# One-hots four groups ahead, transposes two groups ahead, the dense stage in pieces of six products: a graph kernel on one core

## The chip, the cores and the metric

The kernel runs on one core of one Trainium2 chip. The metric is device time in microseconds (us), the median of several timed runs, without the profiler. A profile is one further execution with the hardware profiler recording; its time is given apart wherever it is used.

## The reference

A graph of 6250 nodes (rows of 256 float32 values) and 100,000 edges, each with a source, a destination and one of 8 types. The edges come sorted by destination, and destinations are 6250 u² for uniform u, so low node numbers have many more edges than high ones. Three relational graph layers, then a layer norm, an attention stage and another layer norm:

```python
for l in range(3):
    xr = jnp.einsum('nd,rde->rne', x, W_rel[l])          # 8 matrices of 256x256
    msg = xr[edge_type, src]                             # 100000 x 256
    agg = jax.ops.segment_sum(msg, dst, num_segments=6250)
    x = relu(agg + x @ W_root[l] + bias[l])
x = layernorm(x_in + x)
# attention: for the first 6250 edges, softmax over 4 heads of leaky_relu(alpha_l + alpha_r),
# times the transformed row of the edge's destination, summed over heads, copied to all heads
x = layernorm(x + attention(x))
```

The sum over a node's edges and the product with W_rel can be swapped: first add up, for every destination and type, the source rows, then multiply each of the 8 sums by its matrix. The kernel does that.

## The kernel before, in words

**Tables.** At the start `tables()` turns the edge lists into tables in SBUF: `idx` (the source of each edge), `key` (the column of an edge's type and destination within its tile's window) and `pos` (where a tile's window lies). The edges make 782 tiles of 128. Four consecutive tiles are a *group* (`GT = 4`); a layer has 197 groups, and one step of its loop, `i`, handles one.

**What a step does with a group.** GpSimd fetches the source rows of each tile by an indirect DMA of 128 rows of 1 KB (`gather`, L425), four of them per group, into one of 8 message buffers (`mp`, `bufs=8`). VectorE compares an iota with the keys and so makes the *one-hot* matrices of the group's four tiles in one operation (`onehot`, L409), each 128 edges by 8 types x W destinations; W falls from 26 to 6 along the edge list, since low nodes have more edges per node. TensorE multiplies message by one-hot (`windows`, L442): per tile two products, one for each half of the 256 features, which add up the rows of all edges with the same destination and type in a PSUM bank (`ps_w`, five banks). VectorE adds each tile's result into the ring `S[f]` at a run-time offset (`add`, L454). An fp32 matmul appears in the trace as two records, so a group of four tiles makes 16 window records.

**Two rings.** The edge tiles are split into two halves. `S[0]`, for the upper half of the edges, holds the sums of 4 node tiles of 128 nodes; `S[1]`, for the lower half, holds 3. A group of the upper half touches ring 0, one of the lower half ring 1. `pl.order()` interleaves the two, from the end of each half backwards. Which one-hots are wide differs: in the profile's shapes, a window of a tile has 208 to 144 columns in the one half and 144 to 48 in the other. One node tile is shared between both halves: its part from the lower half is kept aside (`hold`).

**The dense stage.** When the last group that can reach a node tile has been added (`ready`), the tile's row block `xin` has been fetched (`load_rows`), is transposed on TensorE (`turn`, L477) and copied to SBUF by ScalarE as `xT` (L479). In the next step, right behind the next windows, `dense` does 18 products with 256 columns: 2 with W_root (L504) and 16 with W_rel (L507), all into the one PSUM bank `pd`; they are 36 records. One step later `finish` adds the bias (L519), applies relu (L522) and stores the rows in DRAM, where the next layer's gathers read them, and ScalarE clears the tile's place in the ring (`clear`, L514). At most one node tile is handled by `dense` in a step. There are 49 node tiles, so 147 dense tiles in the three layers.

**Order.** The three layers run under a manual schedule: each engine carries out its instructions in the order in which the program emits them, and waits where an operand isn't ready. In the loop's order a step emits: row loads, gathers, position loads on VectorE, the one-hot of the *next* group, `finish` of the tile done in the step before, this group's windows, the dense stage of a tile, this group's adds, and the turn of a tile that has just become ready:

```python
    for i in range(NG + 5):
        ...
        nxt = onehot(i + 1) if i + 1 < NG else None
        ...
            wins = windows(i, msg, oh)
        for f, j, xT in turned[:1]:
            fin.append((f, j, dense(f, j, xT)))
        turned = turned[1:]
        if i < NG:
            add(i, wins, vals)
```

The list `done[f]` names the node tiles whose dense stage has been emitted. An add to a ring declares that it has no conflict with their dense reads if its window lies in other node tiles of the ring; the offset is known only at run time, so an add without that declaration is ordered behind every earlier read of the ring, and a later read behind it.

After the three layers comes `attention()`, which the change doesn't touch.

Of the kernel before, what the change touches and what calls it, by code (L numbers as in the profile page):

```python
# [10 lines left out]
F32 = mybir.dt.float32  # L11
# [8 lines left out]
P = 128  # L20
# [2 lines left out]
NS = (4, 3)  # L23
PAD = 32
MARGIN = 800
LEAD = 6
GWIN = 256
GK = 8
# [3 lines left out]
class Plan:  # L32
# [29 lines left out]
    def order(self):  # L62
# [3 lines left out]
        b = [[t for t in k if t < self.TM] for k in g if k[0] < self.TM]  # L66
        n = max(1, len(b) - LEAD)
        seq, k = [], 0
# [7 lines left out]
    def high(self, t):  # L76
        return max(self.N * ((P * (t + 1) + MARGIN) / self.E) ** 2, 127.0)

    def low(self, t):
        return self.N * (max(0.0, P * t - MARGIN) / self.E) ** 2 - 1.0  # L80

# [48 lines left out]
def fast(tc, const, pl, x, xs, src, dst, edge_type, w_rel, w_root, bias, weight,  # L130
         attn_l, attn_r, out, flag):
    nc = tc.nc
    N, D = x.shape
    E = src.shape[0]
    L, R = w_rel.shape[0], w_rel.shape[1]
    H, DH = attn_l.shape
    KC = D // P
    NT, T, CH, WMAX = pl.NT, pl.T, pl.CH, pl.WMAX
    KR = KC * R

    with ExitStack() as top:
        tab = top.enter_context(tc.tile_pool(name="tab", bufs=1))
        ident = tab.tile([P, P], F32, name="ident")
        idx = tab.tile([P, CH * P], I32, name="idx")
        key = tab.tile([P, CH * P], F32, name="key")
        pos = tab.tile([1, CH * P], I32, name="pos")
        iota_p = tab.tile([P, 1], F32, name="iota_p")
        eps = tab.tile([P, 1], F32, name="eps")
        bias_b = tab.tile([P, L, D], F32, name="bias_b")
        w1x = tab.tile([P, KC, D + 2 * H], F32, name="w1x")  # L150
        altab = tab.tile([P, NT, H], F32, name="altab")

        psi = top.enter_context(tc.tile_pool(name="psi", bufs=1, space=PSUM))
        iota = psi.tile([P, R * WMAX], F32, name="iota")

        dram = top.enter_context(tc.tile_pool(name="lanes", bufs=1, space=DRAM))
        lane = dram.tile([NT * P], I32, name="lane")
        with tc.tile_pool(name="ps_p", bufs=2, space=PSUM) as ps_p:
            tables(tc, pl, ps_p, src, dst, edge_type, ident, idx, key, pos, iota, iota_p,
                   lane, flag, R, H)  # L160
        y = dram.tile([NT * P, D], F32, name="y")

        with ExitStack() as s:
            wp = s.enter_context(tc.tile_pool(name="wp", bufs=2))
            sp = s.enter_context(tc.tile_pool(name="sp", bufs=1))
            mp = s.enter_context(tc.tile_pool(name="mp", bufs=8))
            op = s.enter_context(tc.tile_pool(name="op", bufs=3))
            xp = s.enter_context(tc.tile_pool(name="xp", bufs=3))
            ps_w = s.enter_context(tc.tile_pool(name="ps_w", bufs=5, space=PSUM))
            ps_d = s.enter_context(tc.tile_pool(name="ps_d", bufs=1, space=PSUM))  # L170
            ps_t = s.enter_context(tc.tile_pool(name="ps_t", bufs=1, space=PSUM))


            S = [sp.tile([P, KR, n * P + PAD], F32, name=f"S{f}") for f, n in enumerate(NS)]

            hold = {j: sp.tile([P, KR, P], F32, name=f"hold{j}") for j in sorted(pl.shared(pl.TM))}

            nc.vector.memset(eps, EPS)
            for t in S:
                nc.scalar.memzero(t)  # L180
            nc.sync.dma_start(bias_b, bias.rearrange("l d -> (l d)").partition_broadcast(P))
            fold_weights(tc, xp, w1x, weight, attn_l, attn_r)

            def load_w(l):
                wr = wp.tile([P, KC, R, D], F32, name="wr")
                wo = wp.tile([P, KC, D], F32, name="wo")
                for k in range(KC):
                    nc.scalar.dma_start(
                        wr[:, k], w_rel[l, :, k * P:(k + 1) * P, :].rearrange("r p e -> p r e"))
                    nc.scalar.dma_start(wo[:, k], w_root[l, k * P:(k + 1) * P, :])  # L190
                return wr, wo

            groups = pl.order()

            ready = {}
            for i, (f, g) in enumerate(groups):
                for j in pl.reach(g):
                    ready[f, j] = i

            with tc.manual_schedule():  # L200
                nxt = load_w(0)
                for l in range(L):
                    wr, wo = nxt
                    if l + 1 < L:
                        nxt = load_w(l + 1)
                    layer(tc, pl, l, l == L - 1, groups, ready, S, hold, idx, key, pos, iota, ident,
                          wr, wo, bias_b, x, xs, eps, w1x, altab, y,
                          mp, op, xp, ps_w, ps_d, ps_t, H)

        attention(tc, pl, lane, dst, idx, iota_p, ident, eps, w1x, altab, y, out, H)  # L210
# [178 lines left out]
def layer(tc, pl, l, final, groups, ready, S, hold, idx, key, pos, iota, ident, wr, wo, bias_b, x, xs,  # L389
          eps, w1x, altab, y, mp, op, xp, ps_w, ps_d, ps_t, H):  # L390
    nc = tc.nc
    N, D = x.shape
    KC = D // P
    R = wr.shape[2]
    NT = pl.NT
    LAST = N - (NT - 1) * P
    NG = len(groups)
# [4 lines left out]
    def rows(j):  # L402
        return P if j < NT - 1 else LAST

    def onehot(i):
        g = groups[i][1]
        w = R * pl.W[g[0] // P]
        oh = op.tile([P, GT, R * pl.WMAX], F32, name="oh")
        nc.vector.tensor_tensor(  # L409
            oh[:, :len(g), :w], iota[:, :w].unsqueeze(1).to_broadcast([P, len(g), w]),  # L410
            key[:, g[0]:g[-1] + 1].unsqueeze(2).to_broadcast([P, len(g), w]), ALU.is_equal)
        return oh
# [51 lines left out]

    def load_rows(j):
        n = rows(j)
        t = xp.tile([P, D], F32, name="xin")
        if n < P:
            nc.vector.memset(t, 0.0)
        nc.sync.dma_start(t[:n], table[j * P:j * P + n, :])  # L470
        return t

    def turn(t):

        pt = ps_t.tile([P, 4 * P], F32, name="pt")
        for k in range(KC):
            nc.tensor.transpose(pt[:, k * P:(k + 1) * P], t[:, k * P:(k + 1) * P], ident)  # L477
        xT = xp.tile([P, KC, P], F32, name="xT")
        nc.scalar.copy(xT.rearrange("p k n -> p (k n)"), pt[:, :D])  # L479
        return xT  # L480

# [16 lines left out]
        clear(1, j)  # L498

    def dense(f, j, xT):  # L500
        pd = ps_d.tile([P, 512], F32, name="pd")
        s = cols(f, j)
        for k in range(KC):
            nc.tensor.matmul(pd[:, :D], xT[:, k], wo[:, k], start=(k == 0), stop=False)  # L504
        for k in range(KC):
            for r in range(R):
                i = nc.tensor.matmul(pd[:, :D], s[:, k * R + r], wr[:, k, r],  # L507
                                     start=False, stop=(k == KC - 1 and r == R - 1))
                tc.add_to_no_dep_group(f"used{l}_{f}_{j}", i.ins)
        done[f].append(j)  # L510
        return pd

    def clear(f, j):
        i = nc.scalar.memzero(cols(f, j))  # L514
# [38 lines left out]
    last = {}  # L553
# [2 lines left out]
            last[j] = (i, f)  # L556
    fetch = {}
    for j, (i, f) in last.items():
        fetch.setdefault(max(0, i - 3), []).append(j)
    held, turned = {}, []  # L560
    oh = onehot(0)
    fin, log = [], []
    for i in range(NG + 5):
        for j in sorted(fetch.get(i, []), reverse=True):
            held[j] = load_rows(j)
        if i < NG:
            msg = gather(i)
            vals = places(i)
        nxt = onehot(i + 1) if i + 1 < NG else None
        for j, yt in [t for k, t in log if k <= i - 2]:  # L570
            logits(j, yt)
        log = [(k, t) for k, t in log if k > i - 2]
        for f, j, pd in fin:
            yt = finish(j, pd)
            clear(f, j)
            if final:
                log.append((i, (j, yt)))
        fin = []
        if i < NG:
            wins = windows(i, msg, oh)  # L580
        for f, j, xT in turned[:1]:
            fin.append((f, j, dense(f, j, xT)))
        turned = turned[1:]
        if i < NG:
            add(i, wins, vals)
        for f, j in sorted((k for k, r in ready.items() if r == i), key=lambda k: -k[1]):
            fold(f, j)
            if f == 1 and j in late:
                keep(j)
                continue  # L590
            if j in hold:
                nc.vector.tensor_tensor(cols(f, j), cols(f, j), hold[j], ALU.add)
            turned.append((f, j, turn(held.pop(j))))
        oh = nxt
    assert not (turned or fin or log or held)


def layernorm(nc, pool, o, z, n, eps, tag):
# [439 lines left out]
```

## Time and profile before

| | |
|---|---|
| timed, median of 3 | 3210.28 us (3209.51 to 3214.35) |
| profiled execution | 3974.63 us, its span 3972.9 us |
| granted TensorE clock in the profile, mean | 0.842 of full speed |
| busy: TensorE | 3015.1 us (76% of the span) |
| busy: GpSimd | 2251.2 us (57%) |
| busy: VectorE | 1686.3 us (42%) |
| busy: ScalarE | 471.6 us (12%) |
| DMA | 384.09 MB, mean 97 GB/s |
| 1564 + 782 gathers (L425) | 946 and 948 ns each |
| 9384 window records (L442) | 331 ns each |
| 4704 records of W_rel products (L507) | 399 ns each |
| 591 one-hots (L409) | 677 ns each |
| 2346 adds (L454) | 418 ns each |

The profile's page names a group of instructions by line, engine and operation (PE is TensorE, PEld its weight loads, DVE VectorE, ACT ScalarE, POOL GpSimd); L425 is line 425 of the kernel. "Idle before" is the time in which the engine stood just before instructions of the group, and the name behind it is what ended most of it: another engine's instruction, a DMA, "issue" where the profile shows no wait, "remote" where a signal came that it can't put to one instruction. The busy time of a gather is only what GpSimd does for it; the transfer goes on without it. The profiled execution is a good deal longer than the timed ones, so its waits can't be read as parts of the timed 3210 us without further thought.

### The profile page before, as it was taken

The page shows a single profiled execution, that of the slowest core. Times are in us where ns is not written, and L with a number is a line of the kernel's source. Part 1 is how long each engine was busy: PE and PEld are TensorE (multiplying, and loading weights), DVE is VectorE, ACT ScalarE, POOL GpSimd, SP SyncE. Part 2 cuts the span into 40 slices and gives each one's busy share as a digit, 9 for nine tenths or more (in the row PEclk, how much of TensorE's full clock was granted, in tenths as well). Part 3 has the DMA queues.
Part 4 walks back from the last instruction along what each step waited for, and adds up shares of the span by engine and source line. Part 5 has one row for each costly group of instructions (what it writes and reads, how often), then busy time and mean ns, then how long its engine had stood idle before and what let it go on. Part 6 is the DMA issues. An engine that isn't in the chain of part 4 may idle for free. (4 is left out here: it accounts for less than half of the span.)

```text
span 3972.9 us, 45490 instructions
## 1 busy us (share of the span) xinstructions
PE 3015.1 (76%) x15496; PEld 2703.4 (68%) x15497; DVE 1686.3 (42%) x3982; ACT 471.6 (12%) x627; POOL 2251.2 (57%) x2364
## 2 busy tenths in 40 slices
PE   3888888777777588877778776588888888787763
PEld 2787777676666577767667665477777777676652
DVE  4444443333333344444343333245454444433367
ACT  1111111110000011101110000011111111010023
POOL 5556556666663655566666666355555566666501
PEclk9999988887777799988888777789989888887776
DMA  4333333333332333333333333233333333333332
GB/s 140 96 96 98 93 97 97 95 96 98 95 97 81 100 97 96 92 94 100 97 92 97 95 97 93 61 93 103 92 103 99 96 101 100 101 101 98 89 111 91
DMA packets 187277, 384.09 MB, mean 97 GB/s; under 512 B 43807, under 2 KB 110048, under 8 KB 187040
## 3 DMA queue, kind: packets, MB, share of 16 engines
q0 software_dynamic: 112608, 307.65, 26.7%
q1 hardware_dynamic: 66500, 65.97, 5.2%
q10 hardware_dynamic: 7932, 7.48, 0.6%
q8 instruction: 129, 2.11, 0.2%
q14 instruction: 108, 0.88, 0.1%
HBM read 355.27 MB, written 25.65 MB: 96 GB/s over the span
## 5 line engine op out<-in xcount | busy, mean ns | idle before, releaser
L425 POOL DMA_INDIRECT msg<-x,idx x1564 | 1480.1, 946 | 1054.9 <-issue 461.8
L442 PE MATMUL pw<-oh,msg 128*128 128x168 f32 (+6 forms) x9384 | 1585.9, 331 | 569.9 <-issue 453.0
L442 PEld LDWEIGHTS pw<-oh,msg 128*128 128x128 f32 x9384 | 1502.0, 223 | 641.7 <-issue 525.1
L454 DVE TENSOR_TENSOR S<-S,pw 128x224 f32 (+6 forms) x2346 | 980.6, 418 | 1201.2 <-remote 660.3
L507 PE MATMUL pd<-wr,S 128*128 128x256 f32 x4704 | 1135.8, 399 | 52.6 <-issue 47.6
L507 PEld LDWEIGHTS pd<-wr,S 128*128 128x128 f32 x4704 | 954.2, 203 | 223.6 <-issue 69.9
L425 POOL DMA_INDIRECT msg<-in_x_dram,idx x782 | 741.3, 948 | 485.7 <-issue 208.0
L519 DVE TENSOR_TENSOR pd<-pd,bias_b 128x256 f32<-128x256 f32 x147 | 63.6, 432 | 904.6 <-PE pw L442 402.7
L409 DVE TENSOR_TENSOR oh<-iota,key 128x576 f32<-128x576 f32 (+8 forms) x591 | 399.7, 677 | 39.5 <-issue 23.5
L504 PE MATMUL pd<-wo,xT 128*128 128x256 f32 x588 | 214.3, 500 | 126.0 <-ACT xT L479 79.2
L479 ACT COPY xT<-pt 128x256 f32<-128x256 f32 x196 | 72.6, 371 | 1943.5 <-remote 908.4
L514 ACT ACTIVATE S<-S 128x2048 uint32<-128x2048 uint32 x150 | 285.0, 1900 | 0.1
L504 PEld LDWEIGHTS pd<-wo,xT 128*128 128x128 f32 x588 | 130.9, 245 | 154.7 <-ACT xT L479 90.5
L522 ACT ACTIVATE h<-pd 128x256 f32<-128x256 f32 x98 | 37.6, 384 | 949.9 <-DVE pd L519 915.0
L719 POOL TENSOR_TENSOR pd<-yg,td 128x1792 f32<-128x1792 f32 x7 | 28.3, 4049 | 116.1 <-DVE td L717 48.5
L536 ACT ACTIVATE rs<-mv,eps 128x1 f32<-128x1 f32 x49 | 14.4, 295 | 478.5 <-DVE mv L535 464.8
L548 PEld LDWEIGHTS pt<-w1x,xT 128*128 128x128 f32 x196 | 29.5, 216 | 60.6 <-ACT xT L479 51.9
L548 PE MATMUL pt<-w1x,xT 128*128 128x4 f32 x196 | 33.8, 278 | 48.0 <-ACT xT L479 42.3
L477 PE MATMUL pt<-ident,xin 128*128 128x128 f32 x294 | 63.1, 299 | 2.0 <-issue 2.0
L696 PE MATMUL p<-altab,oh 128*128 128x196 f32 x98 | 32.1, 464 | 35.5 <-DVE sel L703 27.4
L696 PEld LDWEIGHTS p<-altab,oh 128*128 128x128 f32 x98 | 24.4, 271 | 42.9 <-DVE sel L703 32.0
L477 PEld LDWEIGHTS pt<-ident,xin 128*128 128x128 f32 x294 | 45.7, 162 | 7.6 <-issue 3.0
(122 smaller groups left out, 511.3 us busy)
## 6 DMA issues: line engine op xcount, KB each, us to landing
msg<-x,idx POOLq DMA_INDIRECT x1564
msg<-in_x_dram,idx POOLq DMA_INDIRECT x782
x<-h SPq DMA_DIRECT2D x96, 128.0 KB
xin<-x SPq DMA_DIRECT2D x96, 128.0 KB
y<-yt SPq DMA_DIRECT2D x49, 128.0 KB
yg<-y SPq DMA_DIRECT2D x7, 896.0 KB
wr<-in_L_gnn_W_rel_dram ACTq DMA_DIRECT2D x6, 1024.0 KB
xin<-in_x_dram SPq DMA_DIRECT2D x48, 128.0 KB
```

Of the source, the lines that this page charges most:

```text
L409: nc.vector.tensor_tensor(oh[:, :len(g), :w], iota[:, :w].unsqueeze(1).to_broadcast([P, len(g), w]), key[:, g[0]:g[-1] + 1].unsqueeze(2).t ...
L425: nc.gpsimd.indirect_dma_start(out=msg[:, q, :], out_offset=None, in_=table, in_offset=bass.IndirectOffsetOnAxis(ap=idx[:, t:t + 1], axis=0))
L442: nc.tensor.matmul(pw[:, k * w:(k + 1) * w], msg[:, q, k * P:(k + 1) * P], oh[:, q, :w], start=True, stop=True)
L454: ins = nc.vector.tensor_tensor(o, o, pw.rearrange("p (a b) -> p a b", b=W), ALU.add)
L477: nc.tensor.transpose(pt[:, k * P:(k + 1) * P], t[:, k * P:(k + 1) * P], ident)
L479: nc.scalar.copy(xT.rearrange("p k n -> p (k n)"), pt[:, :D])
L504: nc.tensor.matmul(pd[:, :D], xT[:, k], wo[:, k], start=(k == 0), stop=False)
L507: i = nc.tensor.matmul(pd[:, :D], s[:, k * R + r], wr[:, k, r], start=False, stop=(k == KC - 1 and r == R - 1))
L514: i = nc.scalar.memzero(cols(f, j))
L519: nc.vector.tensor_tensor(pd[:, :D], pd[:, :D], bias_b[:, l], ALU.add)
L548: nc.tensor.matmul(pt[:, :H], yT[:, k], w1x[:, k, D + H:D + 2 * H], start=(k == 0), stop=(k == KC - 1))
L696: nc.tensor.matmul(pa[:, :NT * H], oh[0][:, t * P:(t + 1) * P], altab.rearrange("p a h -> p (a h)"), start=True, stop=True)
```

## The change

Three things change in the loop of a layer.

1. One-hots are made four groups ahead (`AHEAD = 4`) and not one: four before the loop, then one for group i + 4 in each step. The pool `op` has 6 buffers, before 3.
2. A node tile is transposed two steps before it becomes ready, not when it does; so its rows are fetched five steps before, not three. `xin` and `xT` have four buffers each, before three.
3. `dense` becomes a generator that yields after every product. A step takes six products from it behind its windows (`PIECE = 6`), or six for each node tile that is waiting if there are more, and stops when a tile's 18 are out; past the last group all go out at once. `done` and `fin` get the tile when its last product is out.

It is for TensorE: that a group's windows find their one-hot made, that the dense stage finds its xT made, and that no node tile's 18 products stand in one block between the windows of two groups. In the changed file the lines are two to four further down (L442 becomes L444, L454 L456, L409 L411, L425 L427, L477 L479, L504 L507, L507 L511, L519 L525).

```diff
+PIECE = 6
+AHEAD = 4
...
-            op = s.enter_context(tc.tile_pool(name="op", bufs=3))
+            op = s.enter_context(tc.tile_pool(name="op", bufs=AHEAD + 2))
...
-        t = xp.tile([P, D], F32, name="xin")
+        t = xp.tile([P, D], F32, name="xin", bufs=4)
...
-        xT = xp.tile([P, KC, P], F32, name="xT")
+        xT = xp.tile([P, KC, P], F32, name="xT", bufs=4)
...
     def dense(f, j, xT):
...
             nc.tensor.matmul(pd[:, :D], xT[:, k], wo[:, k], start=(k == 0), stop=False)
+            yield
...
                 tc.add_to_no_dep_group(f"used{l}_{f}_{j}", i.ins)
+                if k < KC - 1 or r < R - 1:
+                    yield
         done[f].append(j)
-        return pd
+        fin.append((f, j, pd))
...
-        fetch.setdefault(max(0, i - 3), []).append(j)
-    held, turned = {}, []
-    oh = onehot(0)
+        fetch.setdefault(max(0, i - 5), []).append(j)
+    early = {}
+    for j, (i, f) in last.items():
+        early.setdefault(max(0, i - 2), []).append(j)
+    held, turned, xTs = {}, [], {}
+    ohs = [onehot(i) for i in range(min(AHEAD, NG))]
...
-        nxt = onehot(i + 1) if i + 1 < NG else None
+        if i + AHEAD < NG:
+            ohs.append(onehot(i + AHEAD))
...
-            wins = windows(i, msg, oh)
-        for f, j, xT in turned[:1]:
-            fin.append((f, j, dense(f, j, xT)))
-        turned = turned[1:]
+            wins = windows(i, msg, ohs.pop(0))
+
+        n = PIECE * max(1, len(turned)) if i < NG else KC * (R + 1)
+        while turned and n > 0:
+            if next(turned[0], False) is False:
+                turned.pop(0)
+                break
+            n -= 1
         if i < NG:
             add(i, wins, vals)
+        for j in sorted(early.get(i, []), reverse=True):
+            xTs[j] = turn(held.pop(j))
...
-            turned.append((f, j, turn(held.pop(j))))
+            turned.append(dense(f, j, xTs.pop(j)))
```

More of the change, by code (lines that the diff above doesn't have):

```diff
@@ L577, in layer @@
                 log.append((i, (j, yt)))
-        fin = []
+        fin.clear()
         if i < NG:
-            wins = windows(i, msg, oh)
-        for f, j, xT in turned[:1]:
-            fin.append((f, j, dense(f, j, xT)))
-        turned = turned[1:]
+            wins = windows(i, msg, ohs.pop(0))
[5 more added lines that the diff above has]
+            n -= 1
         if i < NG:
             add(i, wins, vals)
+        for j in sorted(early.get(i, []), reverse=True):
+            xTs[j] = turn(held.pop(j))
         for f, j in sorted((k for k, r in ready.items() if r == i), key=lambda k: -k[1]):
@@ L592, in layer @@
                 nc.vector.tensor_tensor(cols(f, j), cols(f, j), hold[j], ALU.add)
-            turned.append((f, j, turn(held.pop(j))))
-        oh = nxt
-    assert not (turned or fin or log or held)
+            turned.append(dense(f, j, xTs.pop(j)))
+    assert not (turned or fin or log or held or xTs)
 def layernorm(nc, pool, o, z, n, eps, tag):
```

## The prediction

> **What bounds the kernel now.** I read the page first, then who waits for whom, then the timeline of three stretches: the start, a layer's middle, a layer's end. The first fact is a mismatch: the profiled run lasts 3974.6 us, the timed median is 3210.28 us. So 764 us of the profile, 24%, are not in the time that is asked for. Which waits are those? The page:
>
> ```profile
> span 3972.9 us, 45490 instructions
> ...
> L425 POOL DMA_INDIRECT msg<-x,idx x1564 | 1480.1, 946 | 1054.9 <-issue 461.8
> L442 PE MATMUL pw<-oh,msg 128*128 128x168 f32 (+6 forms) x9384 | 1585.9, 331 | 569.9 <-issue 453.0
> ...
> L425 POOL DMA_INDIRECT msg<-in_x_dram,idx x782 | 741.3, 948 | 485.7 <-issue 208.0
> ...
> L409 DVE TENSOR_TENSOR oh<-iota,key 128x576 f32<-128x576 f32 (+8 forms) x591 | 399.7, 677 | 39.5 <-issue 23.5
> ```
>
> The columns behind the bar are busy time, mean of one, idle time before. There are 2346 gathers (1564 + 782). Beside them the list of waits:
>
> ```profile
> ACT xT L479 <- remote: 908.4, 52, 74.1
> POOL msg L425 <- issue: 669.8, 2034, 47.5
> ...
> POOL msg L425 <- PE pw L442: 512.5, 178, 19.9
> ```
>
> By this page GpSimd waits for TensorE, and TensorE for one-hots and xT. But a stretch of the timeline near the end of layer 0 shows what kind of waits these are:
>
> ```profile
> 1134.43 0.51 PE L477 MATMUL pt<-ident,xin 128*128 128x128 f32 x2
> ...
> 1134.78 1.88 PE L442 MATMUL pw<-oh,msg 128*128 128x48 f32 x16
> 1135.45 0.45 DVE L454 TENSOR_TENSOR S<-S,pw 128x288 f32 x1 [2.37 <-PE pt L477]
> ...
> 1140.46 0.46 DVE L454 TENSOR_TENSOR S<-S,pw 128x288 f32 x1 [2.43 <-remote]
> ...
> 1143.28 0.37 ACT L479 COPY xT<-pt 128x256 f32<-128x256 f32 x1 [32.88 <-remote]
> ```
>
> The transposes end at 1134.94, and the copy that needs nothing else starts at 1143.28, 8.3 us later; the add of 1140.46 has matmuls that ended before 1134.7 and comes 5.8 us late. The first columns are start and duration, the bracket the idle time before and what ended it. TensorE's signals arrive long after its records. I take this lag for the recording's, since the timed run is 764 us shorter. What cannot be the recording's is the gather's own pace:
>
> ```profile
> 1138.02 0.95 POOL L425 DMA_INDIRECT msg<-in_x_dram,idx  x1 [0.30 <-issue]
> 1139.27 0.95 POOL L425 DMA_INDIRECT msg<-in_x_dram,idx  x1 [0.30 <-issue]
> ```
>
> One every 1.25 us (0.95 + 0.30). It is the same at 14.70, 15.95, 17.24, when TensorE is almost idle and writes few records.
>
> Now the time of a run in which GpSimd never waits inside a layer, all from the timeline. The first gather starts at 10.7; after eight groups it must wait for the first windows, and goes on at 65.57. The other 754 gathers of layer 0 take 754 x 1.25 = 943: 1008. Layer end: 2.3 from the last gather to its windows (1278.5 to 1280.80), 3.5 for a group's windows on the slow clock (as at 1022.52), 17.8 from their end to the next layer's first gather (1258.5 to 1276.3): 1032. Layer 1, 782 x 1.25 = 978: 2010; its end 2.3 + 3.5 + 15.1 (2510.9 to 2526.0): 2031. Layer 2: 3009; 2.3 + 3.5, then 173.5 to the end (3799.3 to 3972.9): 3188, and 2 that the device's time has over the span: 3190. The timed kernel is at 3210. So **GpSimd's gathers bound it**, with some 20 us that this sum does not explain.
>
> [...] the trace has 16 records of 48 columns in 3.48 us at 1022.52 and in 1.88 us at 1134.78, and granted clocks of 0.92 and 0.76 in the first and last third of layer 0.
>
> **The change part by part.**
>
> *One-hots four groups ahead.* Same 591 operations of 0.34 to 1.02 us. In the built program the windows' waits on a one-hot fall from 559 to 10. TensorE gains at most the wait for DVE; without the lag that is small: adds follow the windows tile by tile, so after the last tile come one add (0.57), a load that lies beside it, and a one-hot (0.98), against 1.8 us of the next group's windows. I put 0 to 0.5 us a dense. GpSimd, eight groups ahead, feels none of it. At the start two or three more one-hots (1.02, 0.76, 1.02) stand in DVE's chain before the first windows, some in a 1.28 us gap of it: **+1.5 us**, and gather 29 waits for that.
>
> *Rows fetched five, transposes two groups ahead; four buffers.* Nothing waits but at a layer's end: there the turn (0.65) and its copy (0.37) stand between the last windows and the wo products (1258.29 to 1259.46). They go; the wr products, which wait for the adds (to 1259.65), then start about 1.3 us earlier. Three layer ends: **-4 us**.
>
> *Dense in pieces.* The same 147 x 18 products. Warm, 36 records take 7.9 us (32 in 7.17 at 1238.59, less 0.17 of tail, is 0.219 each), in 2.6 us pieces. New waits come from the ring: `done` gets j only when the last piece is out, so adds to the same ring wait for the piece before them (117 such waits, none before), and a later piece waits for those adds (185 matmuls wait on adds, 99 before). For a tile of ring 0: four adds of 400 columns take 2.59 (236.75) + 0.2 of signal, an estimate, after piece two, against 1.77 us (1.94 at 238.06, less 0.17) of windows of the other ring that TensorE can do meanwhile: it idles about 1.1 us. On ring 1: adds of 224 columns, 1.72 (234.42), against 2.7 (4.47 less 1.77), nothing. Queued behind the waiting product are the next windows, and behind those GpSimd, eight groups later.
>
> Does GpSimd feel it? The tightest part is groups 8 to 70: 63 groups, 315 us of gathers. TensorE's windows of two groups, one of each half, take 4.47 (4.64 at 108.24, less a modelled tail of 0.17), which makes 31.5 x 4.47 = 141, and 20 dense tiles x (7.9 + 0.4 for the turn) = 166: 307. After: plus 14 ring-0 tiles x 1.1 = 15, so 322. That is 7 us more than the gathers give, and the eight buffers hold 40 us less some 7 for landing and windows: about 33. It fits, so inside layers **0**. Sum: +1.5 - 4 = -2.5: **3208 us**.
>
> **Rivals.**
>
> *A, forecast: GpSimd's pace holds, 3208.* For it: the sum of 3190, the constant 1.25, a spread of the times of only 5 us.
>
> *B, the 20 us are real waits of GpSimd for bursts of dense.* Two dense tiles in one go hold TensorE for 16 us warm, 31 cold, close to the 33. In pieces they could not. Then the rest goes too: 3208 - 18 = 3190. For it: the gap; against: the sum of 307 in 315.
>
> *C, slower: the ring's waits overfill the buffers.* With 2 us instead of 1.1 for all 20 tiles TensorE needs 307 + 40 = 347, 32 over, at the limit, and if the clock drops a tenth of the time 15 us a layer more come through: 3208 + 45 = 3253; with half of that 3230. For it: the demand is within 3% of the supply[...].
>
> *D, the waits of the page are largely real* and GpSimd's pace is quicker when not recorded. Then taking the one-hot waits away could give some 4%: 3080. Against: the pace does not depend on load, and 3190 would be a coincidence.
>
> **How the numbers follow.** A 0.47, B 0.25, C 0.20, D 0.08. The likeliest gives 3208. Faster by over 0.2% is under 3203.9: B, D and 0.06 of A: 0.39. Slower is over 3216.7: C and 0.06 of A: 0.26. The same: 0.35. The range leaves out D, half of C and the outermost of B: 3184 to 3236.
>
> **What would show it.** Right: gathers every 1.25 us in the changed profile too, windows never just behind a one-hot, DVE adds waiting for L511's pieces, the layer end a little shorter, and a time within 6 us, whatever the profiled span does (it should fall, since lag hides in fewer waits). Wrong: a time below 3190, which GpSimd's sum forbids unless its pace changes; or GpSimd waiting on windows inside layers beyond what the recording explains, with the time up.

## The result, and the profile after

| | us | ratio to before (95% interval) |
|---|---|---|
| before, median of 4 | 3209.90 (3204.57 to 3214.35) | |
| after, median of 4 | 3181.62 (3180.36 to 3181.82) | 0.9912 (0.9895 to 0.9929) |

The kernel became 28 us faster, where 3208 was predicted and 3184 was the lower end of the range. One thing has to be known to read the numbers: there are executions in which *signals come late* (an instruction starts up to several us after the one that it waits for has ended, in the prediction's timeline the copy of 1143.28 by 8.3 us; all runs on two of the five chips of the experiments were such, of several kernels), and the kernel before then takes 3980 to 4040 us; its profile shown ahead of the prediction was such an execution, while the times above, and the profile after, were not.

The profile of the changed kernel, from the page's first line and its groups (busy, mean of one, idle before and what ended most of it):

```profile
span 3179.8 us, 45124 instructions
...
L427 POOL DMA_INDIRECT msg<-x,idx x1564 | 1486.8, 951 | 522.8 <-issue 475.0
L444 PE MATMUL pw<-oh,msg 128*128 128x168 f32 (+6 forms) x9384 | 1434.5, 311 | 243.0 <-DMA msg<-x,idx 152.0
```

Its list of waits (total, times, longest):

```profile
DVE S L456 <- PE pd L511: 585.5, 117, 7.9
...
POOL msg L427 <- PE pw L444: 44.4, 128, 2.4
...
PE pd L511 <- DVE S L456: 35.3, 79, 0.7
```

The span agrees with the timed runs. GpSimd waits almost nowhere (44.4 us in 128 steps is 0.35 each, and 0.30 is the plain step from one gather to the next). The 117 waits of adds for a piece that the built program foretold are there, to the number, and they cost VectorE 585 us that it had to spare; the pieces wait for adds 79 times, 0.7 us at most.

To compare like with like, the kernel before was profiled again in an execution whose signals come on time. Its page:

```profile
span 3214.4 us, 45490 instructions
...
L425 POOL DMA_INDIRECT msg<-x,idx x1564 | 1490.0, 953 | 546.0 <-issue 479.7
L442 PE MATMUL pw<-oh,msg 128*128 128x168 f32 (+6 forms) x9384 | 1449.0, 316 | 284.2 <-DMA msg<-x,idx 143.1
```

This is what the prediction should have had: a span of 3214, not 3973. GpSimd's list of waits in this execution, first for layer 0 (1 to 994 us):

```profile
POOL msg L425 <- PE pw L442: 14.0, 46, 0.3
POOL msg L425 <- DVE least L280: 9.5, 1, 9.5
```

and for layer 2 (2022 to 3030 us):

```profile
POOL msg L425 <- PE pw L442: 26.7, 48, 5.0
POOL msg L425 <- PE pt L477: 17.0, 13, 3.8
```

In layer 0 no wait for TensorE exceeds the plain step of 0.3 us (the 9.5 us are ahead of the first gather); in layer 2 there are waits of up to 5.0. In both lists the name behind the arrow is only the last signal; what GpSimd waits for is a free message buffer.

With the starts of the gathers in the two timelines the whole difference can be laid out. "After" is here the execution of the changed kernel that was profiled beside the experiments.

| stretch | before, us | after, us |
|---|---|---|
| start to the first gather | 11.3 | 11.2 |
| layer 0, first gather to end of the last | 982.6 | 982.7 |
| to the next layer's first gather | 23.9 | 22.0 |
| layer 1 | 983.5 | 982.5 |
| to the next layer's first gather | 20.7 | 18.5 |
| layer 2 | 1008.0 | 987.5 |
| last gather to the end | 184.6 | 175.5 |
| span | 3214.4 | 3179.9 |

Layers 0 and 1 are the same to about 1 us. **20.5 us come from layer 2, 9.1 from what follows the last gather, 4.1 from the two other layer ends.** (The other profile of the changed kernel, shown above, has 987.1 for layer 2 and 177.7 after the last gather, so the smaller shares are sure to 2 us only.) Layer 2 differs from the others by what it does to a finished node tile: its layer norm, and the *logits*, a transpose (L477), a copy (L479) and two small products (L548), which stand in TensorE's order ahead of the next windows. An experiment below tells the two apart.

### The profile page after: what moved, and what is told of

It is laid out like the page before. It is cut to its first block, busy times and chain, and to the rows that moved or that the text cites. A ratio compares the mean times of both kernels' runs of the same rounds, so it can differ in the third digit from the quotient of the medians.

```text
span 3179.8 us, 45124 instructions
## 1 busy us (share of the span) xinstructions
PE 2739.6 (86%) x15496; PEld 2495.2 (78%) x15497; DVE 1696.7 (53%) x3982; ACT 469.8 (15%) x627; POOL 2259.8 (71%) x2364
## 5 line engine op out<-in xcount | busy, mean ns | idle before, releaser
L427 POOL DMA_INDIRECT msg<-x,idx x1564 | 1486.8, 951 | 522.8 <-issue 475.0
L444 PE MATMUL pw<-oh,msg 128*128 128x168 f32 (+6 forms) x9384 | 1434.5, 311 | 243.0 <-DMA msg<-x,idx 152.0
L444 PEld LDWEIGHTS pw<-oh,msg 128*128 128x128 f32 x9384 | 1376.1, 207 | 296.4 <-issue 153.2
L456 DVE TENSOR_TENSOR S<-S,pw 128x224 f32 (+6 forms) x2346 | 982.0, 419 | 1136.4 <-PE pd L511 585.5
L511 PE MATMUL pd<-wr,S 128*128 128x256 f32 x4704 | 1117.7, 388 | 35.6 <-DVE S L456 35.3
L511 PEld LDWEIGHTS pd<-wr,S 128*128 128x128 f32 x4704 | 900.3, 195 | 167.4 <-DVE S L456 47.8
L427 POOL DMA_INDIRECT msg<-in_x_dram,idx x782 | 743.3, 951 | 247.4 <-issue 219.1
L411 DVE TENSOR_TENSOR oh<-iota,key 128x576 f32<-128x576 f32 (+8 forms) x591 | 399.2, 677 | 36.7 <-issue 19.2
L507 PE MATMUL pd<-wo,xT 128*128 128x256 f32 x588 | 180.1, 435 | 3.3 <-ACT h L528 2.1
L525 DVE TENSOR_TENSOR pd<-pd,bias_b 128x256 f32<-128x256 f32 x147 | 63.3, 431 | 194.0 <-PE pd L511 192.0
L507 PEld LDWEIGHTS pd<-wo,xT 128*128 128x128 f32 x588 | 116.4, 216 | 14.7 <-ACT h L528 2.4
L479 PE MATMUL pt<-ident,xin 128*128 128x128 f32 x294 | 57.8, 279 | 2.9 <-DMA xin<-in_x_dram 2.9
L479 PEld LDWEIGHTS pt<-ident,xin 128*128 128x128 f32 x294 | 42.1, 146 | 13.1 <-DMA xin<-in_x_dram 3.2
```

What stands on the lines that cost most here:

```text
L411: nc.vector.tensor_tensor(oh[:, :len(g), :w], iota[:, :w].unsqueeze(1).to_broadcast([P, len(g), w]), key[:, g[0]:g[-1] + 1].unsqueeze(2).t ...
L427: nc.gpsimd.indirect_dma_start(out=msg[:, q, :], out_offset=None, in_=table, in_offset=bass.IndirectOffsetOnAxis(ap=idx[:, t:t + 1], axis=0))
L444: nc.tensor.matmul(pw[:, k * w:(k + 1) * w], msg[:, q, k * P:(k + 1) * P], oh[:, q, :w], start=True, stop=True)
L456: ins = nc.vector.tensor_tensor(o, o, pw.rearrange("p (a b) -> p a b", b=W), ALU.add)
L525: nc.vector.tensor_tensor(pd[:, :D], pd[:, :D], bias_b[:, l], ALU.add)
```

## The experiments

Ratios are to the kernel before on the same chip at the same time. The kernels stand in groups by question.

### Which part of the change brings it

One-hots ahead, alone:

```diff
-            op = s.enter_context(tc.tile_pool(name="op", bufs=3))
+            op = s.enter_context(tc.tile_pool(name="op", bufs=6))
...
-        nxt = onehot(i + 1) if i + 1 < NG else None
+        if i + 4 < NG:
+            ohs.append(onehot(i + 4))
```

> The kernel before with the one-hots made four groups ahead, and nothing else. Theory H (TensorE lost its time waiting for one-hots that stand behind the previous group's adds on VectorE): this alone brings most of the 28 us, 3180 to 3190 us. Theory P (whole blocks of 18 products hold up the windows) and theory T (transposes and the copy to xT stand in TensorE's way): no gain, 3205 to 3212 us.

> One-hots four groups ahead alone, where signals come on time. Theory P: within 0.3% of before. Theory H: 0.991 to 0.995.

Measured with late signals 1.0075 (1.0050 to 1.0099), and 1.0055 (1.0038 to 1.0072) in a repetition; with signals on time 0.9983 (0.9976 to 0.9990), 3208.5 us beside 3213.7. So the one-hots alone are worth 5 us of the 28. GpSimd still loses 20.7 us in layer 2 (its waits above the plain step, summed along its timeline, here and below).

Early transposes, alone:

```diff
-        fetch.setdefault(max(0, i - 3), []).append(j)
+        fetch.setdefault(max(0, i - 5), []).append(j)
...
+        for j in sorted(early.get(i, []), reverse=True):
+            xTs[j] = turn(held.pop(j))
...
-            turned.append((f, j, turn(held.pop(j))))
+            turned.append((f, j, xTs.pop(j)))
```

> The kernel before with rows fetched five and transposes made two groups ahead, and nothing else. Theory T (the dense stage waits for the copy to xT, which waits for the transposes' late signal): a gain of 1% or more where signals are late; theory P and S: within 0.3% of before, since the wait for xT is exchanged for the wait of the adds.

0.9987 (0.9974 to 1.0000), with signals on time. At most a few us, and 26.1 us lost in layer 2. Theory T spoke of late signals, with which this kernel was not run.

Both, without pieces:

```diff
-PIECE = 6
+PIECE = 18
```

> The changed kernel with 18 products in a piece, so a node tile's dense stage goes out whole behind one group's windows; one-hots four ahead and transposes two ahead stay. Theory P: the gain is gone, 3205 to 3212 us. Theory H or T: the gain stays, 3175 to 3185 us, and a little better than the changed kernel if the waits between pieces and adds cost what I worked out for ring 0 (1.1 us a tile in the tightest part).

> The changed kernel with 18 products in a piece, where signals come on time. Theory P: the gain is gone, within 0.3% of before (3200 to 3215 us), and windows of the third layer at half clock again (28 us of excess with early transposes alone against 3 us with pieces). Theory H (early one-hots would do): the gain stays, 0.991 to 0.994.

With late signals 1.0018 twice (1.0003 to 1.0033 and 1.0006 to 1.0030). With signals on time 0.9978 (0.9968 to 0.9988), 3204.7 us beside 3213.7: just inside the 0.3% of theory P. TensorE's clock in the tightest part of layer 2 is 0.96 of full speed here, 0.97 in the kernel before and 0.99 in the changed kernel (the lines stand further down).

Pieces, alone: the changed `dense`, with the transposes and one-hots as before.

```diff
+        n = 6 * max(1, len(turned)) if i < NG else KC * (R + 1)
+        while turned and n > 0:
...
-            turned.append((f, j, turn(held.pop(j))))
+            turned.append(dense(f, j, turn(held.pop(j))))
```

> The kernel before with the dense stage in pieces of six products, one-hots one group ahead and transposes late as before (xT with four buffers). Theory P: most of the gain, 3180 to 3190 us. Theory H: the pieces add waits of adds for pieces and of pieces for adds, and a one-hot that stands behind a delayed add delays the next windows as well: 3210 to 3240 us. Theory T: 3205 to 3212 us.

> Pieces alone, again, to compare with the changed kernel on the same chip. Theory P: within 0.3% of the changed kernel. Theory S: the changed kernel is 1% or more faster, since with one-hots only one group ahead a one-hot stands behind adds that wait for a piece.

> The changed kernel once more, beside the experiments. If TensorE's signals come late here too (the kernel before near 4025 us): theory P (pieces carry the gain, as pieces alone gave 0.959) expects 0.95 to 0.97 of before; theory S (early one-hots and transposes add to the pieces' gain) expects under 0.94; a theory by which the changed kernel avoids the late signals altogether expects about 3180 us, 0.79. If no signal comes late in these runs: 0.991 of before again.

With late signals pieces gave 0.9591 (0.9562 to 0.9619). With signals on time 0.9927 (0.9907 to 0.9946), 3188.6 us, and the changed kernel beside it 0.9910 (0.9891 to 0.9929), 3183.5. So of the 28 us the pieces alone bring 23; they are 0.16% from the changed kernel, and theory P holds. What one-hots and transposes bring without pieces (0.9978) would cover the rest. How the changed kernel fares with late signals was not measured.

### Why the kernel before lost the time

Four more message buffers in the kernel before:

```diff
-            mp = s.enter_context(tc.tile_pool(name="mp", bufs=8))
+            mp = s.enter_context(tc.tile_pool(name="mp", bufs=12))
```

> The kernel before with 12 message buffers, not 8 (20 us more of gathers ahead). Theory B (GpSimd waits for buffers because TensorE falls behind in bursts and in the tightest stretch): a gain of 15 to 30 us where signals are on time (3180 to 3195 us). If TensorE falls behind all the time, as where signals come late, 20 us at each of three layers at the most, so at most 60 us of 4025 and likely nothing.

0.9932 (0.9912 to 0.9951), 3189.7 us (3180.6 to 3192.1; the profiled execution is the fastest): the gain of the pieces without a single piece. GpSimd's list of waits in layer 2 of this kernel:

```profile
POOL msg L425 <- PE pw L442: 12.5, 41, 0.3
...
POOL msg L425 <- PE pt L477: 4.2, 7, 2.4
```

One wait of 2.4 us is left. So TensorE falls behind for a while and catches up later; the gathers feel it only where it falls behind by more than the buffers hold.

The kernel before without the logits:

```diff
+            nc.vector.memset(altab, 0.0)
...
-            logits(j, yt)
+            pass
```

> The kernel before without the transposes and small products that make the attention logits in the third layer (the table they fill is zeroed instead, so that part of the result is left out). Theory L: GpSimd no longer waits in the third layer, 3180 to 3186 us, as much as the whole change gives. Theory P in its strong form (a block of 36 records is too long whatever else there is): no more than 5 us faster than before.

> The kernel before without the transposes and small products that make the attention logits in the third layer (the table they fill is zeroed instead, so that part of the result is left out). Theory L: where signals come on time GpSimd no longer waits in the third layer, 3180 to 3186 us, as much as the whole change gives. Theory P in its strong form (a block of 36 records is too long whatever else there is): no more than 5 us faster than before.

With late signals 0.9985 (0.9975 to 0.9996); there GpSimd waits in every layer (265, 248 and 263 us in the kernel before), so the logits can't be what decides. With signals on time 0.9915 (0.9898 to 0.9931), 3185.8 us, theory L's number. Its layer 2 takes 983.9 us, as long as the others, and GpSimd's longest wait for windows there is the plain step:

```profile
POOL msg L426 <- PE pw L443: 16.8, 55, 0.3
```

The layer norm is still in this kernel, so the logits, and not it, are what layer 2 has too much.

### Which kind of profile

> The kernel before, profiled once more. Theory 1 (the lag of TensorE's signals belongs to the recording of this program): the profiled span is again near 3970 us, with GpSimd's gathers waiting some 240 us in each layer. Theory 2 (the lag was a chance of that one execution): the span comes near 3210 us, and then its page shows directly where 28 us more than in the changed kernel are lost; GpSimd's waits inside layers should then be 5 to 10 us a layer.

> The kernel before, for its profile where signals come on time. Theory L: no wait of GpSimd over 1 us inside layers 0 and 1, 20 to 30 us of them in layer 2, and a span near 3208 us. The rival, that whole blocks cost something in every layer: 5 to 10 us in each.

The first came with late signals: 4034.5 us, and 15 timed runs of the same kernel beside it at 4018 to 4038; another profile of it, 4029.8, said the same. The second came on time: 3216.2 us, timed runs at 3209.6 to 3217.7, GpSimd's waits 25 us in layer 2 and none above the plain step in layers 0 and 1. In both cases the profiled and the timed runs agree: recording is neither needed for late signals nor enough to bring them. What brings them is open. Two rows of the same stretch of preparation, with late signals:

```profile
24.93 0.15 DVE L288 COPY posf<-at 128x1 f32<-128x1 f32 x1
26.21 0.17 DVE L290 TENSOR_SCALAR qt<-at 128x3 f32<-128x3 f32 x1 [1.13 <-DVE posf L288]
```

and on time:

```profile
20.32 0.14 DVE L288 COPY posf<-at 128x1 f32<-128x1 f32 x1
20.39 0.27 DVE L290 TENSOR_SCALAR qt<-at 128x3 f32<-128x3 f32 x3
```

The second operation follows the first at once, or after 1.13 us. So it is not TensorE's signals alone: VectorE's own come late too.

### What takes the rest, and what stayed open

More buffers on top of the change:

```diff
-            mp = s.enter_context(tc.tile_pool(name="mp", bufs=8))
+            mp = s.enter_context(tc.tile_pool(name="mp", bufs=11))
```

> The changed kernel with 11 message buffers, not 8 (15 us more of gathers ahead). Theory L (only the third layer's tight stretch still overfills the buffers, 4 to 6 us of waits): where signals come on time 3176 to 3180 us, 0.990 of before, no wait of GpSimd over 1 us inside any layer. The rival, that these waits are given back at the layer's end: no different from the changed kernel, 0.991. Where signals come late (before near 4020 us): 0.93 to 0.96, as for pieces alone.

3172.3 us beside 3202.8 (two more executions of the kernel before took over 5200 us and are left out), 0.9904 (0.9885 to 0.9924), on another chip than the 0.9910 of the changed kernel. The two intervals overlap, so the ratio doesn't tell them apart. The trace does show the 4.2 us of waits in layer 2 gone: its gathers take 981.0 us there, as in layers 0 (980.7) and 1 (980.0).

Logits a step later, in the kernel before:

```diff
-        for j, yt in [t for k, t in log if k <= i - 2]:
+        for j, yt in [t for k, t in log if k <= i - 3]:
```

> The kernel before with the logits of a tile made three steps after its finish, not two (yt with four buffers), so that their copy does not stand behind the clear of the tile after it. Theory W (the wait of the logits' products and the half clock after it are what the pieces take away): where signals come on time the waits of these products fall from 36 us to about 20 (0.5 each), few windows of the third layer run at half clock, GpSimd's 25 us of waits in the third layer fall to under 12, and the time to 3190 to 3202 us. Rival I (pieces gain because they interleave windows and products, whatever the logits do): within 0.15% of before, and GpSimd's waits stay at 20 us or more.

This run came with late signals: 1.0112 (1.0085 to 1.0139), with before at 3991 us. In that condition it says that later logits don't help, and nothing about either theory, which were stated for signals on time. That the pieces shorten TensorE's tightest stretch in layer 2 is shown by the lengths in the next section; why they do is argued from traces and not shown by an edit.

## Why the prediction was wrong

*What bounds the kernel.* Right: GpSimd's gathers, at 1.257 us each in both kernels (a layer without waits is 781 steps and one gather of 0.95: 982.6 - 0.95 over 781). Wrong was the reading of the 764 us as made by the recording. The profile came from an execution with late signals; a time of 3974 us was real for it. (The 764 us are 24% of the timed run and 19% of the profile.)

*The sum of 3190 us.* It missed the measured 3210 by 20, and it came that close by luck, since two errors nearly cancel in it. The wait of gather 29, to 65.57, was taken from the late profile; with signals on time it does not happen, and the gather starts at 46.7: 19 us too much. The pace of 1.25 for 1.257 was 2346 x 0.007 = 16 us too little. What was left, and what the sum called unexplained, were the 25 us of GpSimd's waits in layer 2, and a tail 5 us longer than assumed (184.6 for 179.3). So corrected, the sum is 3217, where the profiled execution took 3216.

*The step that failed* is "It fits, so inside layers 0". It priced TensorE's work in the tightest part, groups 8 to 70, by the work of layer 0 and took it for all three. The two traces, by stretches of the timeline (start and end, length, then TensorE's busy time, weight loads, VectorE, ScalarE, GpSimd, granted clock, DMA share, GB/s). The kernel before, from the windows of group 8 to those of group 70, in layers 0, 1 and 2:

```profile
67.45:373.21 305.76, 301.81 (x1754) 281.51 (x1752) 176.50 (x339) 52.51 (x62) 231.41 (x244) 1.00 0.43 122
1064.16:1378.58 314.42, 304.31 (x1753) 283.25 (x1752) 176.90 (x339) 52.50 (x62) 238.15 (x251) 0.99 0.42 122
2068.27:2426.84 358.57, 329.79 (x1873) 302.46 (x1872) 211.45 (x464) 58.22 (x82) 254.46 (x270) 0.97 0.42 121
```

and the changed kernel:

```profile
64.66:374.41 309.75, 303.22 (x1754) 281.38 (x1753) 177.40 (x339) 54.51 (x62) 234.44 (x248) 1.00 0.42 123
1057.66:1374.29 316.63, 305.41 (x1753) 282.97 (x1754) 176.42 (x337) 54.13 (x62) 239.81 (x253) 0.99 0.42 122
2058.67:2403.80 345.13, 325.16 (x1866) 296.30 (x1867) 210.55 (x456) 60.75 (x82) 259.61 (x273) 0.99 0.44 127
```

For layer 0 the estimate of 307 us was good: 306. But layer 2 has some 120 records more in the same groups, and TensorE needs 359 us with its waits, while 62 groups of gathers take 62 x 4 x 1.257 = 312. That is 47 us too long, and the buffers hold about 33 by the prediction's own estimate (32 gathers at 1.25 us are 40, less some 7 for landing and windows; the page of the changed kernel gives 2.8 us from a gather's issue to its landing, and the prediction 4.47 for the windows of two groups). So 14 us should come through; GpSimd lost 25 by the end of the layer. The changed kernel needs 345 us, just what the buffers can take, and loses 4.

The same stretch of layer 2 in the other kernels puts this sum to the test. With early one-hots and transposes but whole blocks, with pieces alone, and without the logits:

```profile
2058.91:2416.77 357.86, 333.73 (x1874) 306.57 (x1872) 211.27 (x464) 57.69 (x83) 254.32 (x269) 0.96 0.42 122
2058.01:2406.87 348.86, 325.81 (x1866) 296.48 (x1867) 209.88 (x455) 59.66 (x82) 258.86 (x273) 0.99 0.43 126
2067.71:2402.01 334.30, 309.74 (x1754) 286.47 (x1753) 207.35 (x443) 50.28 (x62) 253.19 (x267) 0.98 0.45 129
```

| layer 2, signals on time | stretch, us | longer than the gathers' 312 by | buffers hold (estimate) | GpSimd lost in the layer |
|---|---|---|---|---|
| before | 358.6 | 47 | 33 | 25 |
| one-hots alone | 357.2 | 45 | 33 | 21 |
| transposes alone | 356.8 | 45 | 33 | 26 |
| both, whole blocks | 357.9 | 46 | 33 | 23 |
| pieces alone | 348.9 | 37 | 33 | 9 |
| changed kernel | 345.1 | 33 | 33 | 4 |
| before without logits | 334.3 | 22 | 33 | 0 |
| before, 12 buffers | 355.0 | 43 | 53 | 2 |

(Four more buffers hold 16 more gathers, 20 us.) GpSimd loses 21 to 26 us where the third column exceeds the fourth by 12 or more, 9 where it exceeds it by 4, and 4 or less elsewhere; the size of the loss the sum gives only roughly. Early one-hots and transposes leave the stretch as long as it was; the pieces shorten it. So rival B had the right sign and a reason that is not enough: the same blocks stand in layers 0 and 1, where GpSimd loses nothing, and the sum of 307 that was held against it belonged to another layer. Rival B's 31 us for two cold tiles were not measured. An estimate from the profile of before that the prediction read gives about 30: 16 window records of 48 columns took 1.88 us at a granted clock of 1.00 (1134.78 to 1136.50 us) and 3.48 at 0.50 (1022.52 to 1025.90), and 16 x 3.48 / 1.88 is 29.6. That the logits lie on TensorE's path stood in the profile's groups (L548, 196 records), and they were left out.

*Dense in pieces.* The 117 waits came, but not their price. In the tightest part of layer 0 the stretch became 309.75 - 305.76 = 4 us longer than before, and 7 longer than with whole blocks and the rest of the change (302.9), where 15 were estimated: the pieces wait 11 times there, 6.5 us in all and 0.7 us at most, not 1.1 on every tile of ring 0. (The estimate's own terms, 2.59 + 0.2 - 1.77, give 1.0. The 0.2 for a signal was assumed: in the profile of the changed kernel four such adds end at 237.39 and the waiting product starts at 237.45, 0.06 later.)

*What the change saves* in this stretch of layer 2 is 13.4 us of the 358.6, and pieces alone save 9.7. The timeline of before shows one place where they do:

```profile
2179.74 0.38 PE L477 MATMUL pt<-ident,yt 128*128 128x128 f32 x2
...
2179.97 1.89 ACT L514 ACTIVATE S<-S 128x2048 uint32<-128x2048 uint32 x1
...
2181.77 0.35 ACT L479 COPY xT<-pt 128x256 f32<-128x256 f32 x1
...
2182.18 0.61 PE L548 MATMUL pt<-w1x,xT 128*128 128x4 f32 x4 [2.06 <-ACT xT L479]
...
2182.64 4.57 PE L442 MATMUL pw<-oh,msg 128*128 128x200 f32 x16
```

Two node tiles go through `dense` in consecutive steps. The transposes of the first tile's logits end at 2180.12, but their copy stands on ScalarE behind the second tile's clear (L514, 1.89 us), so TensorE is idle for 2.06 us; the windows after that take 4.57 us, at a mean granted clock of 0.67 (last section), where windows of the same shape take 2.87 in the changed kernel (at 2169.77). There a piece lies between the windows and the logits, and at 2175.91 the products wait only 0.46 us for the copy. The waits for this copy in the same stretch, before:

```profile
PE pt L548 <- ACT xT L479: 16.6, 20, 2.1
...
PE pw L442 <- DVE S L454: 5.2, 1, 5.2
```

and after:

```profile
PE pt L554 <- ACT xT L481: 9.2, 19, 0.5
PE pd L511 <- DVE S L456: 4.6, 8, 0.7
```

All waits of TensorE in these stretches sum to 28.7 us before and 20.4 after: 7.4 less for the copy, 5.0 less for one wait at a window, 4.6 more for the pieces, 3.6 more for messages that had not landed, 4.1 less for the rest. The wait at a window lies at the layer's start (2077 us) and has nothing to do with the copy. To these 8 us comes the clock: 0.97 of full speed over 358.6 us lacks 10.8 us of work, 0.99 over 345.1 lacks 3.5, which by estimate is 7 less. Together 15 us, of the 13.4 measured. That the clock comes back because the wait for the copy goes is the author's reading of such rows and was not shown; the run that was to test it came with late signals.

*One-hots and transposes.* That GpSimd "feels none of it" was nearly right (5 us for the one-hots alone, 3 for the transposes). The start's +1.5 us didn't show, since no gather waits there. The layer ends: 1.3 us less each was predicted, and the first two became 1.9 and 2.2 shorter. The third, with the tail, became 9.1 shorter, a size that was missed; pieces alone leave 178.9 us after the last gather, blocks with early transposes and one-hots 183.5, so more of it seems to be the pieces', as far as 2 us of spread between profiles let one say.

*The signs it named.* "A time below 3190, which GpSimd's sum forbids unless its pace changes" came, and the pace had not changed: the sum was wrong.

## What to carry to other kernels

When an engine that runs ahead by a fixed number of buffers sets the pace, do the sum of supply and demand for every layer and stage, with all of its work, and look for the one where the lag outgrows the buffers. There a change of the consumer's order and a few more buffers can buy the same time, as here (3188.6 and 3189.7 us); try the buffers first. And when a profile's span and the timed runs differ by a quarter, take another profile before reading any wait in the first.

## What was not expected of the hardware

The sum of the prediction priced every dense tile at 7.9 us for 36 records. But in layer 2 TensorE's granted clock fell right behind an idle time of 2.06 us, after TensorE had been busy to 2180.12. The stretches around this wait, in the kernel before, and the 5.1 us behind two other waits of 2.06 us for the same copy (the products start at 2234.45 and 2355.26):

```profile
2176.00:2179.70 3.70, 3.70 (x26) 3.44 (x25) 1.43 (x4) 0.00 (x0) 2.79 (x4) 1.00 0.33 99
2179.70:2182.20 2.50, 0.44 (x5) 0.20 (x4) 1.93 (x7) 2.35 (x3) 1.89 (x3) 1.00 0.50 148
2182.20:2187.30 5.10, 5.10 (x22) 4.92 (x22) 2.60 (x7) 0.00 (x0) 3.88 (x5) 0.67 0.67 194
2234.50:2239.60 5.10, 5.10 (x22) 5.00 (x22) 2.54 (x7) 0.00 (x0) 2.45 (x3) 0.67 0.59 157
2355.30:2360.40 5.10, 4.07 (x25) 3.56 (x25) 4.01 (x9) 0.74 (x2) 3.19 (x5) 1.00 0.38 117
```

Three waits of the same length, each with four products of 4 columns behind it, were followed twice by a mean of 0.67 over 5.1 us in which TensorE was busy all the time, and once by 1.00 with 4.07 us busy. So a mean of 0.67 can follow a wait of 2.06 us here, but needn't; what decides it these runs don't show.
